# 1 - a·a of the decays taken as (a - 1)(a + 1) in a fused recurrent layer

## The chip, the core and the metric

The kernel runs on one core of a Trainium2 chip. The metric is the device time of one execution in microseconds (us). A core has five engines that run side by side, each in the order of its own queue, and that wait for one another through semaphores: PE (TensorE, matrix products; its weight loads are shown apart as PEld), DVE (VectorE), ACT (ScalarE), POOL (GpSimd) and SP, which only issues DMAs here. All data is fp32.

## What is computed

Eight sequences of 1024 tokens, 256 features each, are normalised; a gated linear recurrence of 384 channels and a small feed-forward part are added to the input. The part that the change touches is the recurrence:

```python
ig = sigmoid(y @ lru_Wi.T + lru_bi)
rg = sigmoid(y @ lru_Wg.T + lru_bg)
alpha = exp(-8 * softplus(lam) * rg)              # the decay, between 0 and 1
beta  = sqrt(1.0 - alpha ** 2 + 1e-06)
xbeta = beta * ig * y
h[t]  = alpha[t] * h[t - 1] + xbeta[t]
x + (gelu(gate) * h) @ Wo.T + feed_forward(x_normalised)
```

## The kernel before

Features lie on the 128 partitions and tokens along the free axis, so the 384 channels are three tiles of 128 x 1024, numbered m = 0, 1, 2. Three tiles of the recurrence live for one sequence and are used again by the next: `tr` holds the tanh of the decay gate and then the decay itself, `ti` the input gate and then the scaled input, `q` first the factor beta and then the state h.

The products are made from pairs of row blocks by `Group` (L457), which needs seven instead of eight block products per pair: PE fills PSUM banks A and C, ACT copies A into a new bank B (`seed`, L492) and C into SBUF (`five`, L497), and DVE adds them: `fork_c` (L500) reads bank B and adds it to bank C, `fork_d` (L508) reads B again for a fourth result. Between `seed`, `fork_c` and `fork_d` PE goes on adding products into bank B. So the next product into B may not start before `fork_c` has read B. Weights of the gates are `w_l` and their block sums `sum_l`; the groups l0, l1, l2 (`l_group`, L637) make the gates of a sequence. The sums of token blocks that these products need (`token_sum`, L785) are made by POOL from SBUF into SBUF, all recorded at L794; those of the r product are `rsum` and a part of `xr`.

For each m, after the gates have been put through tanh on ACT (L620), this runs: `decay` (ACT, Exp in place in `tr`), `decay_square` (ACT, L891), `decay_rest` (DVE, L894), `beta` (ACT, Sqrt in `q`, L897), `gated_input` (DVE, L901), `scaled_input` (DVE, L904), `recur` (DVE scan, L909), `gated_state` (DVE, L913). The last product with `Wo` follows (L421, in the last sequence L821, and `add_hawk`, L858, adds it to the output tile).

The order on each engine is written out by hand. Every step is given a time by `at` (PE's steps by `pe`), the table `PLACES` overrides the time by the step's name, and the steps are then issued sorted by that time. There is one table for the first sequence, one for the second, one for the five after it and one for the last. The loop `for s in range(B)` (L1089) starts the products of sequence s while DVE and ACT still finish the recurrence of sequence s - 1, so the `decay_rest` of a sequence stands at the end of its own stretch on PE, between the r mixing (`mix`, L811) and the first products of the next sequence (from the table of the five, times in PE steps since the sequence's start):

```python
        "decay_square 1": 76.07, "mix r 1": 76.27, "l1 evict C 0 1": 77.36, "decay_rest 0": 77.77,
        "decay 2": 78.3, "decay_rest 1": 78.58, "stats 6 1": 79.39, "l2 evict A 0 0": 79.64,
        "l2 fork_c": 80.36, "decay_square 2": 80.44, "stats 7 1": 81.17, "decay_rest 2": 81.89,
```

The sequences are counted 0 to 7 here. Those with `decay_rest` at about 149, 224, 299, 375, 450 and 525 us of the profile are 1 to 6; sequence 0 has it at 74 to 87 us and sequence 7, whose tables name it `own decay_rest`, at 586 to 605 us.

Of the kernel before, what the change touches and what calls it, by code (L numbers as in the profile page):

```python
# [9 lines left out]
AF = mybir.ActivationFunctionType  # L10
ALU = mybir.AluOpType
# [230 lines left out]
def kernel(  # L242
# [24 lines left out]
    nc = tc.nc  # L267
# [8 lines left out]
    def fixed(name, shape, dtype=F32):  # L276
        return const.tile([P] + shape, dtype, tag=name, name=name)
# [7 lines left out]
    beta_eps = fixed("beta_eps", [1])  # L285
# [12 lines left out]
    tr, ti, q = fixed("tr", [HC, S]), fixed("ti", [HC, S]), fixed("q", [HC, S])  # L298
# [589 lines left out]
        nc.scalar.activation(tr[:, m, :], tr[:, m, :], AF.Exp, bias=r, scale=r)  # L888

    def decay_square(m):  # L890
        nc.scalar.activation(q[:, m, :], tr[:, m, :], AF.Square)  # L891

    def decay_rest(m):
        nc.vector.tensor_scalar(q[:, m, :], q[:, m, :], -1.0, 1.0, ALU.mult, ALU.add)  # L894

    def beta(m):
        nc.scalar.activation(q[:, m, :], q[:, m, :], AF.Sqrt, bias=beta_eps)  # L897

    def gated_input(m, p=slice(0, S)):

# [54 lines left out]
    def chain(s, b, last):  # L955

        if s + 2 < B:
            at(b + 7.2, deviation, s + 2)
            at(b + 10, inverse, s + 2, 0, TT)
        for m in range(HC):  # L960
            at(b + [7.3, 8.5, 10.5][m], beta, m)
            at(b + [0.5, 1.7, 7.5][m], gated_input, m)
            at(b + [9, 13.2, 19][m], scaled_input, m)
            for h in range(2):
                at(b + [10.3, 15.2, 20.5][m] + 1.5 * h, recur, m, HALVES[h])
            at(b + (43 + m / 2 if last else 32.6 + m / 2), gated_state, s, m)
# [7 lines left out]
    def decays(b):  # L974
        for m in range(HC):
            at(b + [2.2, 2.3, 5.3][m], decay, m)
            at(b + [4, 6, 7][m], decay_square, m)
            at(b + [9.5, 10.5, 11.5][m], decay_rest, m)

    with tc.manual_schedule():  # L980
# [108 lines left out]
        for s in range(B):  # L1089
# [118 lines left out]
            else:  # L1208
# [33 lines left out]
                L, R = HALVES  # L1242
                at(d - 4, decay, 0)
                at(d - 3, decay_square, 0)
                at(d - 2, decay_rest, 0)
                at(d + 8, decay, 1)
                at(d + 8.1, decay_square, 1)
                at(d + 8.5, decay_rest, 1)
                at(d + 10.2, beta, 0)
                at(d + 10.3, beta, 1)  # L1250
                at(d + 17.2, decay, 2)
                at(d + 17.3, decay_square, 2)
# [80 lines left out]
```

## Time and profile before

| | |
|---|---|
| time, three runs | 627.54 us median (627.36 to 628.5) |
| time of the profiled execution | 626.81 us |
| its span, first to last instruction | 625.0 us, 7457 instructions |
| mean granted TensorE clock | 0.999 |
| busy: DVE, ACT, POOL | 530.8, 473.1, 327.7 us |
| `decay_square` L891, ACT, 24 instructions | 25.1 us, mean 1050 ns |
| `beta` L897, ACT, 24 instructions | 27.6 us, mean 1152 ns |
| `mix_before` L805, ACT Copy with a scale per partition, `xr`, 16 instructions | 18.0 us, mean 1138 ns |
| `scaled_input` L904, DVE, two tiles in, 23 of the 24 whole tiles | 31.3 us, mean 1362 ns |

"Busy" is the time in which an engine worked on an instruction. A group of the profile gives a line, the engine, the operation, output<-inputs by their names, the shape, the count, the busy time and the mean of one, then how long the engine had sat idle before such instructions and what released it. A timeline row gives start, duration (both in us), engine, line, operation and shapes; the bracket at its end is idle time before it and its releaser. The chain of waits follows the work that ended last backwards to its start. A duration on DVE or POOL runs from the moment at which the engine took the instruction up, so it also holds what the instruction waits for inside the engine.

### The profile page before, as it was taken

What the parts mean: (1) busy time and instruction counts of PE and PEld (TensorE: products, weight loads), DVE (VectorE), ACT (ScalarE), POOL (GpSimd) and SP (SyncE); (2) the same over time, 40 slices, a digit from 0 to 9 for tenths busy, and PEclk for the clock granted to TensorE, in tenths of its full rate; (3) what the DMA queues carried; (4) which work ended last, traced back from release to release, by engine and by line L of the source; (5) the groups of instructions that cost most, each with busy time, mean ns of one, the idle gap of its engine ahead of it and who ended that gap; (6) DMA issues with size and microseconds to landing.
All of it is one profiled execution on the core that took longest, in us unless ns stands there. A gap on an engine that the chain in (4) does not pass through costs nothing.

```text
span 625.0 us, 7457 instructions
## 1 busy us (share of the span) xinstructions
PE 616.4 (99%) x2539; PEld 369.9 (59%) x2539; DVE 530.8 (85%) x656; ACT 473.1 (76%) x670; POOL 327.7 (52%) x227
## 2 busy tenths in 40 slices
PE   9999999999999999999999999999999999999997
PEld 5465445943459544694447844487445964457466
DVE  5797799989889898898898888988988987789695
ACT  5997999568894789848889398884888749883880
POOL 4997834578134870539507393084911769427000
PEclk9999999999999999999999999999999999999999
DMA  7202500173001720029000380006600044000403
GB/s 269 67 2 28 108 0 1 35 174 63 0 0 46 180 46 1 0 64 197 10 1 1 92 177 0 2 2 142 128 0 1 14 122 69 0 0 1 68 20 116
DMA packets 35334, 35.10 MB, mean 56 GB/s; under 512 B 2784, under 2 KB 34784, under 8 KB 35296
## 3 DMA queue, kind: packets, MB, share of 16 engines
q1 hardware_dynamic: 26560, 25.83, 14.9%
q0 software_dynamic: 8320, 8.39, 9.0%
q8 instruction: 20, 0.33, 0.2%
q10 hardware_dynamic: 416, 0.41, 0.2%
q14 instruction: 18, 0.15, 0.1%
HBM read 19.94 MB, written 8.39 MB: 45 GB/s over the span
## 4 chain that ended last, share of the span: by engine, by line
PE 91%; DVE 5%; ACT 2%; DMA 1%; issue 0%; DVEq 0%; ACTq 0%
PE bank L415 62%; PE bank L421 23%; PE bank L821 4%; PE bank L578 1%; DMA out_dram<-side 1%; DVE xk L811 1%; DVE st L718 1%; DVE y L877 1%; DVE q L894 1%; DMA xt<-in_x_dram 1%; DVE xr L811 0%; DVE bank L500 0%; ACT g L612 0%; DVE q L909 0%; PE bank L745 0%
## 5 line engine op out<-in xcount | busy, mean ns | idle before, releaser
L415 PE MATMUL bank<-y,w_l 128*128 128x512 f32 x288 | 137.9, 593 | 0.0
L877 DVE SCALAR_TENSOR_TENSOR y<-u,par,y 128x1024 f32<-128x1024 f32 x72 | 106.8, 1506 | 0.2
L492 ACT COPY bank<-bank 128x512 f32<-128x512 f32 x76 | 43.7, 575 | 65.9 <-PE bank L415 48.2
L415 PEld LDWEIGHTS bank<-y,w_l 128*128 128x128 f32 x288 | 53.0, 190 | 58.6 <-issue 57.1
L500 DVE TENSOR_TENSOR bank<-bank,five 128x512 f32<-128x512 f32 x76 | 52.6, 694 | 34.9 <-PE bank L415 24.9
L415 PE MATMUL bank<-ysum,sum_l 128*128 128x512 f32 x144 | 71.5, 595 | 0.8 <-DVE bank L500 0.8
L415 PE MATMUL bank<-xsum,sum_u 128*128 128x512 f32 x138 | 69.4, 592 | 0.0
L794 POOL TENSOR_TENSOR tr<-g 128x512 f32<-128x512 f32 x12 | 22.1, 1838 | 79.8 <-ACT u L608 69.2
L794 POOL TENSOR_TENSOR ysum<-y,ysum 128x512 f32<-128x512 f32 x16 | 28.4, 1778 | 57.7 <-PE bank L415 50.1
L794 POOL TENSOR_TENSOR xsum<-ysum 128x512 f32<-128x512 f32 x12 | 16.0, 1347 | 65.9 <-PE bank L421 58.8
L497 ACT COPY five<-bank 128x512 f32<-128x512 f32 x76 | 43.7, 583 | 6.1 <-PE bank L415 3.8
L415 PEld LDWEIGHTS bank<-ysum,sum_l 128*128 128x128 f32 x144 | 26.8, 190 | 36.1 <-issue 28.2
L415 PE MATMUL bank<-xnT,w_u 128*128 128x512 f32 x92 | 47.0, 592 | 0.0
L620 ACT ACTIVATE tr<-bank,half_b 128x512 f32<-128x512 f32 x48 | 32.1, 679 | 16.1 <-PE bank L415 16.1
L415 PEld LDWEIGHTS bank<-xsum,sum_u 128*128 128x128 f32 x138 | 25.7, 190 | 29.7 <-issue 27.7
L421 PE MATMUL bank<-w_o,g 128*128 128x128 f32 x288 | 37.0, 275 | 0.0
L620 ACT ACTIVATE ti<-bank,half_b 128x512 f32<-128x512 f32 x48 | 31.5, 684 | 7.1 <-PE bank L415 6.9
L421 PEld LDWEIGHTS bank<-w_o,g 128*128 128x128 f32 x288 | 35.0, 192 | 2.9 <-issue 2.9
L740 ACT ACTIVATE xt<-xt,mv,std 128x256 f32<-128x256 f32 x60 | 34.0, 595 | 1.0 <-DVE mv L731 1.0
L894 DVE TENSOR_SCALAR q<-q 128x1024 f32<-128x1024 f32 x24 | 33.4, 1409 | 1.3 <-ACT q L891 1.2
L901 DVE SCALAR_TENSOR_TENSOR ti<-ti,y 128x1024 f32<-128x1024 f32 (+1 forms) x25 | 31.1, 1263 | 3.9 <-ACT ti L620 3.9
L904 DVE SCALAR_TENSOR_TENSOR ti<-ti,q 128x1024 f32<-128x1024 f32 (+1 forms) x25 | 32.7, 1308 | 0.7
(164 smaller groups left out, 1476.1 us busy)
## 6 DMA issues: line engine op xcount, KB each, us to landing
side<-in_x_dram POOLq DMA_DIRECT2D x8, 1024.0 KB, 9.3
xt<-in_x_dram SPq DMA_DIRECT2D x28, 256.0 KB, 4.6
xnT<-xk SPq DMA_DIRECT2D x96, 64.0 KB, 2.0
out_dram<-side SPq DMA_DIRECT2D x12, 512.0 KB, 4.6
xt<-in_x_dram SPq DMA_DIRECT2D x1, 1024.0 KB, 5.6
out_dram<-side SPq DMA_DIRECT2D x4, 256.0 KB, 2.2
out_dram<-side SPq DMA_DIRECT2D x8, 128.0 KB, 1.7
w_l<-in_lru_wg_dram SPq DMA_DIRECT2D x1, 576.0 KB, 6.1
```

Source lines behind the costliest of these rows:

```text
L415: nc.tensor.matmul(banks[b], weight, tokens, start=start, stop=True, skip_group_check=True)
L421: nc.tensor.matmul(banks[b][:, p], tokens[:, p], weight, start=start and j == 0, stop=True, skip_group_check=True,)
L492: nc.scalar.copy(banks[bank["B"]], banks[bank["A"]])
L497: nc.scalar.copy(self.five, banks[bank["C"]])
L500: nc.vector.tensor_tensor(banks[bank["C"]], banks[bank["B"]], self.five, ALU.add)
L620: nc.scalar.activation(dst[:, m, HALVES[h]], src, AF.Tanh, bias=half_b[:, b + m : b + m + 1], scale=0.5)
L740: nc.scalar.activation(xa, xa, AF.Identity, bias=m, scale=r)
L794: nc.gpsimd.tensor_tensor(dst[o], a, b, ALU.subtract)
L877: nc.vector.scalar_tensor_tensor(y[:, m, :], u[:, m, k : k + S], column(COL_CONV_W + k * HC + m), y[:, m, :], ALU.mult, ALU.add,)
L894: nc.vector.tensor_scalar(q[:, m, :], q[:, m, :], -1.0, 1.0, ALU.mult, ALU.add)
L901: nc.vector.scalar_tensor_tensor(ti[:, m, p], ti[:, m, p], 1.0, y[:, m, p], ALU.add, ALU.mult)
L904: nc.vector.scalar_tensor_tensor(ti[:, m, p], ti[:, m, p], 0.5, q[:, m, p], ALU.mult, ALU.mult)
```

## The change

`decay_square` writes a + 1 into `q` instead of a·a, with Copy and a bias of 1. `decay_rest` reads two tiles instead of one, and leaves (a - 1)(a + 1) = a·a - 1 in `q`, the negative of what it left before. `beta` takes the sign back with its scale. No step is added, removed or moved, and no tile is added.

```diff
     def decay_square(m):
-        nc.scalar.activation(q[:, m, :], tr[:, m, :], AF.Square)
+
+        nc.scalar.activation(q[:, m, :], tr[:, m, :], AF.Copy, bias=1.0)
 
     def decay_rest(m):
-        nc.vector.tensor_scalar(q[:, m, :], q[:, m, :], -1.0, 1.0, ALU.mult, ALU.add)
+
+        nc.vector.scalar_tensor_tensor(q[:, m, :], tr[:, m, :], -1.0, q[:, m, :], ALU.add, ALU.mult)
 
     def beta(m):
-        nc.scalar.activation(q[:, m, :], q[:, m, :], AF.Sqrt, bias=beta_eps)
+        nc.scalar.activation(q[:, m, :], q[:, m, :], AF.Sqrt, bias=beta_eps, scale=-1.0)
```

## The prediction

> **What bounds the kernel.** I read the page's busy shares, then its chain of waits, then the groups, then the timelines of DVE, POOL and the weight loads around each L894.
>
> ```profile
> PE 616.4 (99%) x2539; PEld 369.9 (59%) x2539; DVE 530.8 (85%) x656; ACT 473.1 (76%) x670; POOL 327.7 (52%) x227
> ...
> PE 91%; DVE 5%; ACT 2%; DMA 1%; issue 0%; DVEq 0%; ACTq 0%
> ...
> L877 DVE SCALAR_TENSOR_TENSOR y<-u,par,y 128x1024 f32<-128x1024 f32 x72 | 106.8, 1506 | 0.2
> ...
> L894 DVE TENSOR_SCALAR q<-q 128x1024 f32<-128x1024 f32 x24 | 33.4, 1409 | 1.3 <-ACT q L891 1.2
> ```
>
> PE is the bound. It has next to no idle time, so a DVE delay costs only where PE waits for DVE, but there it costs in full: PE has no slack later to win it back. The reader should doubt the mean of 1409 ns. The view of this one line gives minimum, median and maximum, and the timeline tells why:
>
> ```profile
> L894 DVE TENSOR_SCALAR q<-q x24: 661/1752/1766, 73.9 to 605.3; 128x1024 f32<-128x1024 f32 x24
> ...
> 605.28 0.69 DVE L894 TENSOR_SCALAR q<-q 128x1024 f32<-128x1024 f32 x1
> ...
> 599.86 1.22 DVE L904 SCALAR_TENSOR_TENSOR ti<-ti,q 128x1024 f32<-128x1024 f32 x1
> ```
>
> With POOL idle (5 of 24) L894 takes 0.66 to 0.69 us. The other 19 start while a POOL instruction runs, and hold a wait. Sequence 2, DVE, POOL and weight loads:
>
> ```profile
> 224.15 3.44 DVE L894 TENSOR_SCALAR q<-q 128x1024 f32<-128x1024 f32 x2
> ...
> 228.05 0.67 DVE L500 TENSOR_TENSOR bank<-bank,five 128x512 f32<-128x512 f32 x1
> ...
> 223.10 2.25 POOL L794 TENSOR_TENSOR rsum<-xr 128x512 f32<-128x512 f32 x1
> 225.44 1.60 POOL L794 TENSOR_TENSOR rsum<-xr,rsum 128x512 f32<-128x512 f32 x1
> ...
> 228.78 0.30 PEld L415 LDWEIGHTS bank<-ysum,sum_l 128*128 128x128 f32 x2 [0.60 <-DVE bank L500]
> ```
>
> POOL's rsum ends at 223.10 + 2.25 = 225.35; the first L894 (224.15 to 225.91) ends 0.55 us later. The second POOL row ends at 227.04, the second L894 at 227.58, again 0.55 later. POOL's own row ends 1.13 us after the L894 in front of it. The two engines take turns: each waits for the other's whole instruction. Last, the weight load for PE's next product into bank B was released by L500, 0.06 us after that ended. PE lost 0.04 us there, so the cover is exactly used up.
>
> **DVE part (L894).** The new instruction reads two SBUF tiles. Alone, its nearest row is L904, two tiles and an immediate: 1.22 us against 0.68, **+0.53**. Beside POOL the nearest row is L877:
>
> ```profile
> 185.85 1.26 POOL L794 TENSOR_TENSOR tr<-g,tr 128x512 f32<-128x512 f32 x1
> 187.09 2.25 POOL L794 TENSOR_TENSOR xsum<-ysum,xsum 128x512 f32<-128x512 f32 x1
> ...
> 186.30 1.91 DVE L877 SCALAR_TENSOR_TENSOR y<-u,par,y 128x1024 f32<-128x1024 f32 x1
> ```
>
> This L877 ends at 188.21, and the first POOL row had ended at 187.11: 1.10 us before (1.08 where I read the times to the nanosecond). POOL's xsum, taken up meanwhile, ends at 189.34, again 1.13 after the DVE instruction in front of it. So the turns stay and each of DVE's is 1.08 instead of 0.55 us: **+0.53** too, and POOL's next instruction starts its turn 0.53 later.
>
> Here a rule weighs in. The Trainium skill, page "VectorE: DVE Perf Modes", section "Rules for kernel authors", says of chained DVE operations to minimise their number, not their semaphores. By count the change is free: 24 before, 24 after, +0.0 us. The rows say that the form decides: by them DVE gets 24 x 0.53 = 12.8 us more work. The same page's perf-mode tier table speaks against the change: fp32 with one source runs two elements a cycle, two-tensor operations one. I take the rows.
>
> **Where the 0.53 reaches PE.** A pair of L894 stands in front of L500 in six sequences.
> - Sequence 1: L500 already released PE late (PE lost 0.44 us at 153.5). Both ops count: 2 x 0.53 = 1.06.
> - Sequences 2 to 5: L500 moves from 228.72 (end) to 229.78. PE loses 0.04 to 0.08 there today, so all of it comes on top: 4 x 1.06 = 4.24.
> - Sequence 6 (525 us): L500 ends at 529.44, 0.20 before its weight load at 529.64. Late by 1.06 it lets the load go at 530.56. The second product of such a late pair starts 0.53 after the first load (seen at 153.48/154.02 and 228.78/229.31), so at 531.09, which is 0.59 after its present 530.50.
> - Sequence 0: one L894 alone in front of L500 (ends 75.19; +0.53 gives a load at 75.78, second product 76.31 against 76.03: 0.28). The two others delay DVE by 1.6 in all; its idle gaps at 96.40 (0.41) and 105.06 (0.62) take most, and the L508, scan, L500 run that already releases PE at 108.62 ends 0.13 later still: 0.4 in all.
> - Sequence 7: the first L894 (585.67) costs PE 0.12, since its L500 had 0.14 to spare. The second (596.07): a DVE gap of 0.17 takes a part, L508 releases PE 0.05 late. The third (605.28): DVE is 0.37 late, its gap there takes 0.09, it adds 0.53, and gaps of 0.03 and 0.04 follow: 0.74 late at L913, which ends at 612.26 now and releases a weight load at once: 0.73. Together 0.9.
>
> Sum: 1.06 + 4.24 + 0.59 + 0.4 + 0.9 = **7.2 us**.
>
> The third L894 of sequences 1 to 6 (at 229.18) delays L508 by 1.6 us in all, to 232.7; PE needs it at 232.75 + 1.06. This cover is 1.1 us. After it DVE waits for PE anyway (2.07 us idle before the L500 at 236.88), so the lateness ends there. If that cover were gone: 0.53 per sequence, 3.2 us. POOL's rsum and xr come 1 to 1.6 us later; after 229.94 POOL has nothing until 244.52, so nothing queued behind them is late.
>
> **ACT parts.** Copy with an immediate bias: the trace has Square with immediates at 1.045 us and Copy with one per-partition scale at 1.138 (L805); Sqrt with one per-partition bias is 1.15 and Exp with two such operands 1.24. So 0.09 for an operand of that kind, and none here: 1.045, as before; at worst 24 x 0.09 = 2.2 us of ACT, of which only the two L894 that wait for ACT (585.67, 605.28) could pass on 0.2; below 1.045 at most the same 0.2 could be gained. The scale -1 in Sqrt is an immediate, whose place exists already (scale 1): 0, and its bounds are the same. Order, semaphore waits and table loads of all engines stay: `tr` is written by ACT before `q`, and DVE's wait for `q` covers both.
>
> **Time.** Span 625.0 + 7.2 = 632.2; the profiled run has 1.8 around its span, so 634.0. The median lies 0.73 above that run: **634.7 us**.
>
> **Rivals.**
> - *Cover that I don't see (630.5).* The delays of sequences 2 to 5 vanish, if PE's loss there is less than L500's delay: 7.2 - 4.2 = 3.0. For it: the stall is 0.04 now, and other stalls (0.26 at 186.5, 0.30 at 200.2 and their like) might shrink. Against: those wait on POOL and DVE steps that themselves wait on PE and so move with it. Chance 0.13.
> - *No turn-taking (628, not slower).* If the two-tile form doesn't wait for POOL in this place, it takes 1.22 instead of 1.76: L500 comes 1.1 earlier and PE gets back its 0.44 and 0.23 of sequences 1 to 5; the ends cost their 0.3 and 0.9 still: +0.5. It decides once the pair takes less than its present 3.44 us. For it: some L877 and L811 rows overlap POOL and take 1.28. Against: in these DVE was first, or POOL ended soon; where POOL was first they wait. Page "SBUF — State Buffer", section "Who interferes with whom", also counts both forms as contending. Chance 0.05.
> - *More reaches PE (638).* The third op also, +3.2. For: POOL's later turns. Against: the cover of 1.1. Chance 0.08.
> - *The form isn't what it says (627.5)*: chance 0.02; the program's order shows q<-tr,q.
>
> The main case has 0.72, from 633.5 to 636. The range 631.0 to 637.5 takes in most of the first and a part of the third rival. Under 0.2% (1.3 us) nothing can be told from no change: slower 0.93, same 0.05 (the turn-taking rival and the last one, less the 0.02), faster 0.02.
>
> **What would show it.** DVE's line of q (L896 in the changed kernel) without POOL at 1.22, in pairs at 2.29 each; DVE busy near 543; the weight load behind L500 waiting 1.7 instead of 0.6 us in sequences 2 to 5; ACT's Copy at 1.045. It is wrong if the pair stays near 1.76, or if PE's loss at L500 stays under 0.5.

## The result and the profile after

| | before | changed |
|---|---|---|
| median of four runs each | 627.45 us (626.64 to 628.5) | 634.73 us (633.73 to 635.12) |
| ratio of times, 95% interval | | 1.0113 (1.0099 to 1.0127) |
| span of the profiled execution | 625.0 us | 632.9 us |

The changed kernel is slower by 1.13%. The interval is 6.2 to 8.0 us. First the page of the changed kernel: busy times, the shares of the chain of waits, and two groups.

```profile
PE 618.5 (98%) x2539; PEld 369.6 (58%) x2539; DVE 543.4 (86%) x656; ACT 473.1 (75%) x670; POOL 335.2 (53%) x227
...
PE 83%; DVE 11%; DMA 2%; ACT 2%; issue 1%; SPq 0%; DVEq 0%; ACTq 0%
...
L877 DVE SCALAR_TENSOR_TENSOR y<-u,par,y 128x1024 f32<-128x1024 f32 x72 | 106.2, 1498 | 0.2
...
L896 DVE SCALAR_TENSOR_TENSOR q<-tr,q 128x1024 f32<-128x1024 f32 x24 | 46.1, 1940 | 1.2 <-ACT q L892 1.2
```

The counts are those of before; DVE has 12.6 us more work, and POOL, of which no instruction changed, 7.5 us more: POOL's durations hold its waits for DVE. DVE's share of the chain rose from 5 to 11% (9% in a second profile of this kernel), PE's fell from 91 to 83%. ACT is busy for the same 473.1 us. (The change adds two empty lines to the file and so moves the line numbers: L891, L894, L897, L901, L904, L909, L913 of before are L892, L896, L899, L903, L906, L911, L915 here. L500, L508, L794, L811 and L858 kept theirs.)

The view of the changed DVE line, and of ACT's line ahead of it; the three durations are minimum, median and maximum in ns.

```profile
L896 DVE SCALAR_TENSOR_TENSOR q<-tr,q x24: 1192/2281/2297, 75.3 to 613.0; 128x1024 f32<-128x1024 f32 x24
...
L892 ACT ACTIVATE q<-tr x24: 1040/1044/1067, 72.6 to 611.8; 128x1024 f32<-128x1024 f32 x24
```

The median was 1752 ns and is 2281, so most of the 24 stand in a turn with POOL, each 0.53 us longer. The minimum of 1192 is the instruction alone. Copy takes 1044 ns, and Sqrt (L899) still 1151. The timeline of sequence 2, DVE, POOL and weight loads:

```profile
226.83 4.51 DVE L896 SCALAR_TENSOR_TENSOR q<-tr,q 128x1024 f32<-128x1024 f32 x2
...
231.81 0.67 DVE L500 TENSOR_TENSOR bank<-bank,five 128x512 f32<-128x512 f32 x1
...
232.94 1.84 DVE L896 SCALAR_TENSOR_TENSOR q<-tr,q 128x1024 f32<-128x1024 f32 x1
...
225.78 2.25 POOL L794 TENSOR_TENSOR rsum<-xr 128x512 f32<-128x512 f32 x1
228.11 2.14 POOL L794 TENSOR_TENSOR rsum<-xr,rsum 128x512 f32<-128x512 f32 x1
...
232.53 0.30 PEld L415 LDWEIGHTS bank<-ysum,sum_l 128*128 128x128 f32 x2 [1.70 <-DVE bank L500]
```

The pair took 3.44 us and takes 4.51. POOL's rsum ends at 228.03, and the second POOL row at 230.25; DVE's second instruction ends at 231.34, 1.09 us after that. Two short instructions of the statistics and L500 follow at once, as they did before, and the weight load goes 0.05 us after L500's end, having waited 1.70 instead of 0.60 us. So the whole 1.07 us of the pair is handed on to PE.

To find where PE lost time, I took each of its products in both traces and subtracted the starts. The difference holds still where PE is not delayed, and jumps where it is:

| stretch (times of before) | jump of PE's lateness, us | forecast |
|---|---|---|
| up to 53 us, ahead of every changed instruction | 1.33 | |
| sequence 0 | 0.28 | 0.4 |
| sequence 1 (153 us) | 1.06 | 1.06 |
| sequences 2 to 5 (229, 304, 379, 455 us) | 4.27 (1.05 to 1.09 each) | 4.24 |
| sequence 6 (530 us) | 0.57 | 0.59 |
| sequence 7 (586 to 621 us) | 0.39 | 0.9 |
| sum without the first row | 6.57 | 7.2 |

The first row isn't the change's doing: nothing has been changed in what runs before 71 us. In the profiled executions of the seven kernels below it came out between -0.36 and +1.81 us against the same run of before, in kernels with the old form of the line as well. I call it the start's scatter and take it off in what follows. It begins with the 17 products on the tile `warm` with which PE starts (L1004, here L1006); the first of them take 0.63 us each and the last 0.38. Fifteen of them in the run of before, then in the changed kernel:

```profile
1.18 5.55 PE L1004 MATMUL bank<-five 128*128 128x512 bf16 x15 [1.18 <-DVE five L981]
```

```profile
1.18 6.03 PE L1006 MATMUL bank<-five 128*128 128x512 bf16 x15 [1.18 <-DVE five L983]
```

In the run of before, 10 of the 17 took the long time; in the two executions that started earlier it was 7 and 8, in the six that started later 11 to 14. What sets the moment of the switch stayed open, and how the 0.48 us here grows to the 1.15 us of lateness at 10 us was not followed. The unprofiled times fall into two clumps too (on the chip of the first four experiments the kernel before took 626.2 to 626.8 us 17 times and 627.4 to 628.7 us 35 times), so a median moves with the share of each; that would fit the starts, but is not shown to be the same thing.

The change itself costs 7.90 - 1.33 = 6.57 us in this pair of traces.

### The profile page after: what moved, and what is told of

Same layout as the page of the kernel before. It is cut to its first block, busy times and chain, and to the rows that moved or that the text cites. A ratio compares the mean times of both kernels' runs of the same rounds, so it can differ in the third digit from the quotient of the medians.

```text
span 632.9 us, 7457 instructions
## 1 busy us (share of the span) xinstructions
PE 618.5 (98%) x2539; PEld 369.6 (58%) x2539; DVE 543.4 (86%) x656; ACT 473.1 (75%) x670; POOL 335.2 (53%) x227
## 3 DMA queue, kind: packets, MB, share of 16 engines
q1 hardware_dynamic: 26560, 25.83, 14.6%
## 4 chain that ended last, share of the span: by engine, by line
PE 83%; DVE 11%; DMA 2%; ACT 2%; issue 1%; SPq 0%; DVEq 0%; ACTq 0%
PE bank L415 53%; PE bank L421 23%; PE bank L821 4%; DVE q L896 4%; DVE xr L811 1%; DMA xt<-in_x_dram 1%; DVE bank L500 1%; PE bank L1006 1%; DVE st L718 1%; PE bank L578 1%; DVE bank L508 1%; DMA out_dram<-side 1%; DVE y L877 1%; DVE xk L811 0%; DVE mv L720 0%
## 5 line engine op out<-in xcount | busy, mean ns | idle before, releaser
L500 DVE TENSOR_TENSOR bank<-bank,five 128x512 f32<-128x512 f32 x76 | 52.6, 694 | 32.7 <-PE bank L415 23.1
L794 POOL TENSOR_TENSOR tr<-g 128x512 f32<-128x512 f32 x12 | 22.1, 1839 | 80.3 <-ACT u L608 68.7
L794 POOL TENSOR_TENSOR ysum<-y,ysum 128x512 f32<-128x512 f32 x16 | 28.5, 1779 | 57.7 <-PE bank L415 50.1
L794 POOL TENSOR_TENSOR xsum<-ysum 128x512 f32<-128x512 f32 x12 | 17.0, 1436 | 64.8 <-PE bank L421 58.8
L896 DVE SCALAR_TENSOR_TENSOR q<-tr,q 128x1024 f32<-128x1024 f32 x24 | 46.1, 1940 | 1.2 <-ACT q L892 1.2
L903 DVE SCALAR_TENSOR_TENSOR ti<-ti,y 128x1024 f32<-128x1024 f32 (+1 forms) x25 | 31.0, 1262 | 3.8 <-ACT ti L620 3.8
L906 DVE SCALAR_TENSOR_TENSOR ti<-ti,q 128x1024 f32<-128x1024 f32 (+1 forms) x25 | 32.7, 1307 | 0.7
```

Of the source, the lines that this page charges most:

```text
L500: nc.vector.tensor_tensor(banks[bank["C"]], banks[bank["B"]], self.five, ALU.add)
L794: nc.gpsimd.tensor_tensor(dst[o], a, b, ALU.subtract)
L896: nc.vector.scalar_tensor_tensor(q[:, m, :], tr[:, m, :], -1.0, q[:, m, :], ALU.add, ALU.mult)
L903: nc.vector.scalar_tensor_tensor(ti[:, m, p], ti[:, m, p], 1.0, y[:, m, p], ALU.add, ALU.mult)
L906: nc.vector.scalar_tensor_tensor(ti[:, m, p], ti[:, m, p], 0.5, q[:, m, p], ALU.mult, ALU.mult)
```

## The experiments

The theory to test is the prediction's: the longer turn of DVE, in front of a step that PE waits for, is what costs. The rivals are DVE's total load, ACT's new instructions, and POOL's longer rows. The time of each kernel stands beside runs of the kernel before on the same chip; "in the trace" means PE's lateness at its last products less the start's scatter.

### ACT's part alone

The changed kernel with DVE's old line:

```diff
-        nc.vector.scalar_tensor_tensor(q[:, m, :], tr[:, m, :], -1.0, q[:, m, :], ALU.add, ALU.mult)
+        nc.vector.tensor_scalar(q[:, m, :], q[:, m, :], -1.0, 1.0, ALU.mult, ALU.add)
```

> The two ACT edits alone: Copy with a bias of 1 into q and Sqrt with scale -1 stay as in the changed kernel, but DVE keeps its one-tile instruction (it leaves -a in q, so the output is not the reference's). Theory of the longer DVE turn: the ACT edits cost nothing, so 627.5 us within 0.6 of the kernel before; Copy at 1.045 us like Square, DVE's 24 instructions at 0.68 alone and 1.76 in the pairs, PE's loss behind L500 0.04 to 0.08 us in sequences 2 to 5. Rival, ACT pays: above 629, with Copy or Sqrt longer than before (1.14 us if the bias is an operand per partition).

Measured: 627.49 us against 627.69, ratio 1.0 (0.999 to 1.0011); 0.02 us in the trace. The view of DVE's line:

```profile
L896 DVE TENSOR_SCALAR q<-q x24: 660/1751/1765, 75.2 to 606.6; 128x1024 f32<-128x1024 f32 x24
```

It is the row of before again (661/1752/1766), with ACT's Copy at 1044 ns and the scale in Sqrt. ACT's edits cost nothing and gain nothing; all of it is in DVE's line.

### The same line behind the step that PE waits for

The changed kernel with one instruction of the pair, `decay_rest 1`, moved behind `l2 fork_c` (L500), in two tables:

```diff
-        "decay_square 1": 76.01, "mix r 1": 76.75, "l1 evict C 0 1": 77.36, "decay_rest 1": 78.25,
+        "decay_square 1": 76.01, "mix r 1": 76.75, "l1 evict C 0 1": 77.36, "decay_rest 1": 80.38,
...
-        "decay 2": 78.3, "decay_rest 1": 78.58, "stats 6 1": 79.39, "l2 evict A 0 0": 79.64,
+        "decay 2": 78.3, "decay_rest 1": 80.38, "stats 6 1": 79.39, "l2 evict A 0 0": 79.64,
```

> The changed kernel with one step moved: in sequences 1 to 6 decay_rest 1 is issued behind l2 fork_c (L500) instead of in front of it. All 24 two-tile instructions stay. Theory of the longer turn in front of L500: L500 now has one such instruction ahead of it, ends before PE needs it, and the 5.9 us of sequences 1 to 6 go, with the 0.67 us that the kernel before lost there: about 627.5 us, no PE loss behind L500 in sequences 1 to 5, DVE busy still near 543 us. Rival, DVE's 12.6 us more work as such or lateness that reaches PE elsewhere: stays above 632 us.

Measured: ratio 0.9995 (0.9987 to 1.0004), 626.9 us; -0.07 us in the trace. The busy line of its page, and sequence 2 in its timeline:

```profile
PE 616.2 (99%) x2539; PEld 369.9 (59%) x2539; DVE 539.2 (86%) x656; ACT 473.3 (76%) x670; POOL 342.3 (55%) x227
```

```profile
223.58 2.29 DVE L896 SCALAR_TENSOR_TENSOR q<-tr,q 128x1024 f32<-128x1024 f32 x1
...
226.34 0.68 DVE L500 TENSOR_TENSOR bank<-bank,five 128x512 f32<-128x512 f32 x1
226.93 1.22 DVE L896 SCALAR_TENSOR_TENSOR q<-tr,q 128x1024 f32<-128x1024 f32 x1
...
227.83 0.19 PEld L415 LDWEIGHTS bank<-ysum,sum_l 128*128 128x128 f32 x1 [0.24 <-issue]
```

L500 now ends at 227.02, and the weight load at 227.83 waits for no DVE instruction. DVE is still busy 8.4 us longer than before, and POOL 14.6 us longer, and neither costs anything here. That fells the two rivals of total load. The -0.07 us of the trace is a gain of 0.67, which PE had lost behind L500 in sequences 1 to 5 before the change, against a loss of 0.20 in sequence 0 and 0.40 in sequence 7, where nothing was moved. DVE's busy time is 539.2 and not near 543, because the moved instruction now mostly came before POOL's turn and took 1.22 us.

### POOL out of the way

The changed kernel with POOL's sums for the r product moved behind the first sum for the o product, so that nothing on POOL runs beside the pairs of sequences 2 to 5:

```diff
-        "token_sum r 0": -1.17, "gated_input 0": -0.0, "beta 0": 0.33, "token_sum r 1": 1.42,
+        "token_sum r 0": 16.01, "gated_input 0": -0.0, "beta 0": 0.33, "token_sum r 1": 16.02,
...
-        "u0 seed": 1.56, "beta 1": 2.24, "scaled_input 0": 2.58, "u0 five": 3.47, "token_sum r 2": 4.01,
+        "u0 seed": 1.56, "beta 1": 2.24, "scaled_input 0": 2.58, "u0 five": 3.47, "token_sum r 2": 16.03,
...
-        "token_sum r 3": 6.63, "l2 evict B 1 0": 7.56, "recur 0 R": 7.79, "l2 evict D 1 1": 9.16,
+        "token_sum r 3": 16.04, "l2 evict B 1 0": 7.56, "recur 0 R": 7.79, "l2 evict D 1 1": 9.16,
```

> The changed kernel with POOL's four sums for the r product moved in POOL's order behind the first sum for the o product, in the five sequences of the middle table, so that POOL is idle while the pairs of sequences 1 to 5 run. Theory of turns: the paired instructions take 1.22 us each instead of 2.29, L500 comes earlier than in the kernel before, PE loses nothing behind it in sequences 1 to 5; about 628.7 us, since sequence 6 and the two ends keep their loss, plus what the moved sums cost where they now run. Rival, the two-tile instruction is slow in this place for a reason of its own: still 2.29 us each and about 634.7 us.

Measured: 629.34 us, ratio 1.0028 (1.0014 to 1.0041), 1.13 us in the trace. The view of the line, then sequence 2 in the timeline:

```profile
L896 DVE SCALAR_TENSOR_TENSOR q<-tr,q x24: 1192/1212/2294, 75.6 to 607.9; 128x1024 f32<-128x1024 f32 x24
```

```profile
225.98 2.35 DVE L896 SCALAR_TENSOR_TENSOR q<-tr,q 128x1024 f32<-128x1024 f32 x2
...
228.80 0.67 DVE L500 TENSOR_TENSOR bank<-bank,five 128x512 f32<-128x512 f32 x1
...
230.23 0.19 PEld L415 LDWEIGHTS bank<-ysum,sum_l 128*128 128x128 f32 x1 [0.24 <-DVE mv L720]
```

The same two instructions in the same order take 2.35 us as a pair instead of 4.51, and L500 no longer holds the load: the 0.24 us in the bracket is the usual distance between loads of this row of products, the same as in the second experiment. So the turn with POOL is shown, not only read: the two-tile form costs 1.2 us by itself and 2.29 behind a POOL sum. The expectation was 628.7. Sequences 2 to 5 went as it said. In sequence 1 the first L896 still met another POOL sum (2.29 us), and PE lost the 0.44 us there that it had lost before the change: that part missed. The moved sums bring turns of their own elsewhere (DVE's busy time is still 543.3 us), which cost PE 0.05 to 0.09 us per sequence at the o product. What is left of the loss is mostly sequence 6 (0.59 us) and the two ends (0.15 and 0.39 us).

### The new form at the two ends only

The kernel before, with all three new steps in sequences 0 and 7 and the old ones in between. `at_an_end` counts the calls and is true in these two; the square and `beta` choose in the same way:

```diff
-        nc.vector.tensor_scalar(q[:, m, :], q[:, m, :], -1.0, 1.0, ALU.mult, ALU.add)
+        if at_an_end("rest", m):
+            nc.vector.scalar_tensor_tensor(q[:, m, :], tr[:, m, :], -1.0, q[:, m, :], ALU.add, ALU.mult)
+        else:
+            nc.vector.tensor_scalar(q[:, m, :], q[:, m, :], -1.0, 1.0, ALU.mult, ALU.add)
```

> The new form of all three steps in sequences 0 and 7 only, the old one in 1 to 6. The forecast had 0.4 us for sequence 0 and 0.9 for sequence 7: 628.8 us. The trace of the changed kernel reads as 0.27 and 0.38: 628.1 us, PE rows of the last sequence losing 0.10 behind L500 and 0.27 at the product that waits for g (L913). Rival, the whole loss is at the ends (nothing is lost in the middle): 634.

Measured: ratio 1.0005 (0.9998 to 1.0013), so +0.3 us with -0.1 to +0.8. The medians, 628.57 against 627.69 us, are 0.9 apart, but they move with the starts. In the trace it is 0.66: 0.24 in sequence 0, and in sequence 7 0.12 behind L500 and 0.27 at the product that waits for g. The forecast's 0.4 + 0.9 = 1.3 lies outside of the interval and is twice the trace's value. The ends were priced too high, as the table of jumps says too.

### The changed kernel once more

> The changed kernel once more, with more runs. PE's rows of its trace give the change's own cost as 0.27 (sequence 0) + 1.06 + 4.27 (2 to 5) + 0.57 (6) + 0.38 (7) = 6.55 us; the other 1.34 us of its longer span lie before 54 us, ahead of every changed instruction. If that start is a scatter of the executions, the ratio to the kernel before is 1.0104; if the start is part of the change, 1.0126; the forecast's sum of 7.2 would be 1.0115.

Measured: 633.75 us, ratio 1.0109 (1.0093 to 1.0125). In the trace 6.49 us, with a start of +1.81. (The expectation's 6.55 us is 6.57 when the starts are taken to the nanosecond; sequence 7 has 0.39.) The interval holds the sum of the trace (1.0104) as well as the forecast's 7.2 (1.0115): the times alone can't tell them apart. The two traces can, with 6.57 and 6.49.

### No such instruction at all

Since 1 - a·a + 1e-06 is Sqrt's argument with scale -1 and bias 1 + 1e-06, DVE's step can be left away and ACT's square kept. The kernel before with

```diff
-        nc.vector.tensor_scalar(q[:, m, :], q[:, m, :], -1.0, 1.0, ALU.mult, ALU.add)
+        pass
...
-        nc.scalar.activation(q[:, m, :], q[:, m, :], AF.Sqrt, bias=beta_eps)
+        nc.scalar.activation(q[:, m, :], q[:, m, :], AF.Sqrt, bias=beta_eps, scale=-1.0)
...
-        nc.gpsimd.memset(beta_eps, BETA_EPS)
+        nc.gpsimd.memset(beta_eps, 1.0 + BETA_EPS)
```

> The kernel before with DVE's decay_rest left out: Square stays, and the root itself takes scale -1 and a bias of 1.000001, so beta = sqrt(-a a + 1.000001). DVE has 24 instructions less (33 us of its busy time). Theory of L500: PE wins back only what it lost behind L500 in sequences 1 to 5, 0.67 us, and at most 0.4 more at 108.6 us: 626.5 to 627. Rival, DVE's load as such costs time: well under 626, in proportion to 33 us less.

Measured: 627.24 us against 626.81, ratio of the runs 0.9998 (0.9989 to 1.0007), so no change that the times can show; -0.67 us in the trace. The busy line of its page:

```profile
PE 616.5 (98%) x2539; PEld 370.6 (59%) x2539; DVE 499.7 (80%) x632; ACT 472.8 (76%) x670; POOL 318.4 (51%) x227
```

DVE has 24 instructions and 31 us less, and what comes of it is what PE lost behind L500 before, no more. This is the other side of the second experiment: 8 us more on DVE cost nothing there, 31 us less bring 0.1% at most here.

### The old form behind the step

The kernel before with the two lines of the table moved as in the second experiment.

> The kernel before, one-tile DVE instruction, with decay_rest 1 issued behind l2 fork_c in sequences 1 to 6. Theory of L500: the 0.67 us lost behind L500 in sequences 1 to 5 go: 626.9 us, ratio 0.9989. Rival: the moved step makes something else late and the time stays at 627.6 or above.

Measured: ratio 0.9992 (0.9982 to 1.0001), 626.46 us; -0.70 us in the trace. That is a gain of 0.1%, and the interval still holds no change. It equals that of the kernel without the instruction, as it should if all that the old form cost was its place in front of L500. None of these kernels measurably beats the one before.

## Why the prediction was right, and where its sum was off

- **Bound and cover: right.** PE is the bound, and the cover in front of L500 was used up: sequences 2 to 5 gave 4.27 us for 4.24, and sequences 1 and 6 the forecast's numbers within 0.02.
- **+0.53 per instruction: right.** Alone 1.19 to 1.23 us, in the pairs 2.28 to 2.30. DVE's busy time grew by 12.6 us for 24 x 0.53 = 12.7 (not 12.8). By the rule of the Trainium skill (page "VectorE: DVE Perf Modes", section "Rules for kernel authors") on the number of operations alone the change is free: the count stayed at 656. The form decided, as the tier table that the prediction set against that rule has it.
- **ACT at nothing: right** (first experiment), with Copy at 1044 ns for 1045.
- **The third instruction is covered: right.** It took 1.84 us in sequence 2, and sequences 2 to 5 lost nothing beyond the pair's share. The rival of 638 fell.
- **The rivals of 630.5 and 628 fell.** No other wait of PE shrank to make up for the delays, but for 0.10 us in sequence 0 (below), and the two-tile form does wait for POOL in this place. (The range of 631.0 to 637.5 was said to take in most of the first rival, yet its 630.5 lies outside.)
- **The terms of the two ends were mis-sized.** The forecast's sum has 0.4 for sequence 0 and 0.9 for sequence 7; they were 0.28 and 0.39. In sequence 7 the step that failed is the one that took each idle gap of DVE at its shown length: "a DVE gap of 0.17 takes a part", "its gap there takes 0.09", "gaps of 0.03 and 0.04 follow". In this tail, DVE's instructions that follow each other at once start 0.08 to 0.09 us before the end recorded for the one ahead. The tail of the changed kernel on DVE:

```profile
603.70 1.22 DVE L896 SCALAR_TENSOR_TENSOR q<-tr,q 128x1024 f32<-128x1024 f32 x1
604.83 1.22 DVE L903 SCALAR_TENSOR_TENSOR ti<-ti,y 128x1024 f32<-128x1024 f32 x1
605.96 0.68 DVE L858 TENSOR_TENSOR side<-side,bank 128x512 f32<-128x512 f32 x1
...
613.01 1.22 DVE L896 SCALAR_TENSOR_TENSOR q<-tr,q 128x1024 f32<-128x1024 f32 x1
...
619.56 0.68 DVE L915 TENSOR_TENSOR g<-g,q 128x512 f32<-128x512 f32 x1
```

L896 ends at 604.92 and L903 has started at 604.83; L903 ends at 606.05 and L858 has started at 605.96. In the trace of before, the same L858 started 0.17 after L901's end at 597.89:

```profile
596.67 1.22 DVE L901 SCALAR_TENSOR_TENSOR ti<-ti,y 128x1024 f32<-128x1024 f32 x1
598.05 0.69 DVE L858 TENSOR_TENSOR side<-side,bank 128x512 f32<-128x512 f32 x1 [0.17 <-PE bank L821]
```

So the slack in that gap was 0.17 + 0.08 = 0.25 us, and the starts show it: against before, L903 is late by 8.16 and L858 by 7.91. The gaps of 0.09, 0.03 and 0.04 likewise held 0.18, 0.12 and 0.12. DVE's lateness over PE's then runs 0.53 - 0.25 - 0.18 + 0.53 - 0.12 - 0.12 = 0.39 us at L915 instead of 0.74 (the starts show 0.35). The weight load behind it went 0.35 later, and PE's products from the next one on were 0.27 late instead of 0.73. With the 0.12 that the sequence's first L896 cost, as forecast, that is the 0.39 of the table. The 0.05 at L508 was nothing by the same slack.

Sequence 0 is another case. The two gaps of 0.41 and 0.62, taken as shown, would leave 0.57 of the 1.6, and the sum has 0.4. PE lost 0.37 behind the L500 that followed the first L896 (0.27 to 0.37 in the five profiled executions with the new form there) for a forecast of 0.28, and then, where the forecast has a further loss of 0.13, got 0.10 back at the weight load of 108.62, in all five. The step that failed is the one that left the scan in front of that load's L500 at its length. The scan and the POOL sum in front of it, before:

```profile
105.67 2.31 DVE L909 TENSOR_TENSOR_SCAN q<-tr,q,ti 128x512 f32<-128x512 f32 x1
...
105.62 1.27 POOL L794 TENSOR_TENSOR xsum<-ysum,xsum 128x512 f32<-128x512 f32 x1
```

In the changed kernel DVE comes to the scan while POOL is still at the sum before that one:

```profile
107.85 1.65 DVE L911 TENSOR_TENSOR_SCAN q<-tr,q,ti 128x512 f32<-128x512 f32 x1
...
106.17 2.24 POOL L794 TENSOR_TENSOR xsum<-ysum 128x512 f32<-128x512 f32 x1 [6.04 <-ACT ysum L660]
```

The scan ends 1.09 us after the POOL sum in both, but in the second it began later in POOL's turn and waited less. It took 1.65 us in all five executions, and 2.31 to 2.32 in the three with the old form (before, the first and the last experiment). Another scan, 8 us earlier on DVE, took 0.48 us longer in its turn (1.69 for 1.21); the two together are most of what lies between 0.13 lost and 0.10 won. So PE can win a little back after all, where a later DVE instruction falls into another turn.

- **The median fell on 634.73 for a forecast of 634.7.** That is closer than the sum deserves. The sum was 0.6 us too high, and the run that it was set against began 1.3 us earlier than the profiled run of the changed kernel did. How the starts of the unprofiled runs lay is not known, so a median this near is in part luck.

## What to carry to other kernels

Price a tensor operation by its form and its neighbours, not by its count: here, one operation for one operation cost 0.53 us more each time. Then look at what stands behind it on its engine: in front of a step that releases the bound engine, all of that is paid once the cover is used up, and behind that step nothing. When slack is read from idle gaps, add the overlap that back-to-back instructions on that engine show.

## What the runs showed of the hardware that was not expected

- **Slack on DVE is larger than its idle gaps**, by the 0.08 to 0.09 us above. Over the four gaps of the tail this made 0.39 us of lateness out of a forecast 0.74.
- **The turn costs POOL as well.** Its busy time went from 327.7 to 335.2 us with the changed kernel and to 342.3 with the moved one, without one POOL instruction changed. The Trainium skill, page "SBUF — State Buffer", section "Who interferes with whom", names both forms as contending with GpSimd. The traces agree: DVE's instruction ends 0.55 us (one tile) or 1.08 us (two tiles) after POOL's, for 128 x 1024 fp32.
- **A turn that falls differently can pay back.** The scan in sequence 0 took 1.65 instead of 2.31 us because DVE came to it later.
- **The start scatters.** PE's lateness at 53 us ran from -0.36 to +1.81 us over eight profiled executions, against the same run of before, and 7 to 14 of PE's first 17 products took 0.63 instead of 0.38 us. That is as large as many a change; comparing PE's products one by one takes it out, comparing spans doesn't.
